# The gathers of the expert layers take their row numbers from sixteen columns that VectorE fills, and come one per piece or cycle

## The chip, the cores and the metric

The kernel runs on one core of a Trainium2 chip. The metric is the device time of one execution in microseconds (us): the median of the runs. Engines are called PE (TensorE), PEld (its weight load), DVE (VectorE), ACT (ScalarE), POOL (GpSimd) and SP (SyncE) in the profile.

## The reference, cut to what matters

Four transformer layers run in turn over 16 sequences of 256 tokens with 128 features (4096 tokens). Each has an attention and a second half, both behind a normalisation that is scaled and shifted by a condition. The second half of layer 0 and of layer 1 is a mixture of eight experts of which each token uses two. For layer 0, cut:

```python
gout = xt @ Wg.T
topv, topi = jax.lax.top_k(gout, 2)
w = jax.nn.softmax(topv, axis=-1)
comb = jnp.einsum('tke,tk->te', jax.nn.one_hot(topi, 8), w)
h = jax.nn.silu(xt @ W1[e] + b1[e]) * (xt @ W2[e] + b2[e])     # for each expert e
out = sum over e of comb[:, e] * (h @ W3[e] + b3[e])
```

Layer 1's mixture has one relu matrix product in the place of the two gated ones, and a small attention of its own before it. A token needs the results of its two experts only, which is what the kernel's lists use.

## The kernel before, in words

The tokens are in 8 blocks of 512, four blocks to a half. Layer 0 and layer 1 do their mixtures in the same four steps.

*Lists.* While the preceding attention runs, the gate of each block is worked out, and each token's row is written (scattered) by GpSimd into the list of each of its two experts, in DRAM (`rows`). When a half's lists are complete, `pieces` writes two tables: `piece`, which rows and which expert each piece has, and `origin[half]`, a 128x2x16 integer tile that says for each token in which row of the results its first and its second expert's result will stand.

*Pieces.* `sparse` runs over 2 x 23 pieces of 256 rows. For piece n it loads the rows and the expert's weights (two pieces ahead, SP queue), turns the rows (`ps_in` to `l_x`, VectorE), multiplies by the first matrices (`ps_hid` to `s`), multiplies by the second (`ps_out` to `l_o`, ScalarE) and stores the 256 results in DRAM (`done`, ACT queue).

*Sums.* `tail(blk)` calls `list_sums(blk)`: for each of four groups of 128 tokens and each of the two experts, an indirect DMA issued by GpSimd gathers 128 rows of `done` into `list_rows`, by the numbers in one column of `origin[half]` (L1619, L1620). That makes 8 gathers a block, 64 a layer. `list_rows` has room for two blocks, so block k+2's gathers wait until block k's have been summed. Then the combination weights are transposed and multiplied by the last bias (`wT`), VectorE adds the gathered rows with their weights (`acc`, in layer 1 `list_sums`), and the sums are turned and added to `x`.

*Ticks.* `tail` and the lists' functions are generators that stand in `self.later`; `advance()` steps each of them once and counts `self.tick`. In the pieces it is called three times a piece, in the attention that follows once a step (layer 1, 128 steps) or once a cycle (layer 2's attention of small heads, 138 cycles). In `list_sums` each gather is followed by one `yield`, or two in the pieces. When a tail has written its last gather, the next tail begins (it may begin when the tail two before it has summed). The first tail begins with the 25th piece, when the first half's results are out; the last four need the second half's. The attention of the next layer asks for a block's `x` through `self.tailed`, and would step the generators at once until it has it.

*Order.* Every call is written into one program; the order on each engine is then fixed when the program is compiled, from what is ready when, and with it the semaphores that carry each dependency. In the parts that matter here only the matrix products are pinned to the order in which they are written (`self.strict`); VectorE, ScalarE and GpSimd are pinned too (`self.strict_all`) in layer 0's attention and in layer 3 alone.

Names in the profile: `E` is the attention's exponentials. In layer 1 GpSimd multiplies them by `sm_inv` before TensorE transposes them into `PT`; in layer 2 GpSimd masks them (L1391) and makes `km`, the keys that TensorE starts a unit with (L1259), and `m` is their maxima (VectorE, L1383). `hb` is the normalised block that an attention starts from. `half_below` is a mask that layer 2's attention casts at its start. L230 is the line of a helper that calls VectorE, ScalarE and GpSimd; the matrix products are L273 and L276.

Of the kernel before, what the change touches and what calls it, by code (L numbers as in the profile page):

```python
# [11 lines left out]
I32 = mybir.dt.int32  # L12
# [225 lines left out]
class _Kernel:  # L238
# [522 lines left out]
    def list_tables(self, pool):  # L761
        self.in_pieces, self.listed_halves, self.tailed = False, 0, 0
        self.tails_begun = self.halves_done = self.summed = 0

        room = self.w.tile([P, 4 * BLK], F32, tag="m2", name="list_room")
        self.list_rows = self.w.tile([P, 4, BLK], F32, tag="m1", name="list_rows")
        at = 0

        def take(n):
            nonlocal at  # L770
            at += n
            return room[:, at - n : at]

        rt = take(self.t["route"].shape[-1])
        self.nc.sync.dma_start(out=rt, in_=self.t["route"])
        self.prefix, rest = rt[:, :P], rt[:, P:]
        self.first8, self.step8 = rest[:, :8], rest[:, 8:16]
        self.tri8 = rest[:, 16:80].rearrange("p (e f) -> p e f", f=8)
        self.numbers = rest[:, 80:]
        self.hots, self.two_w, self.place, self.ends, self.piece, self.origin = [], [], [], [], [], []  # L780
        two = lambda: take(32).rearrange("p (i t) -> p i t", i=2)
        eight = lambda: take(256).rearrange("p (i t e) -> p i t e", i=2, e=8)
        self.list_z, self.behind = eight(), take(NPIECE * 8).rearrange("p (k e) -> p k e", e=8)
        self.comb1 = take(NTILE * 8).rearrange("p (t e) -> p t e", e=8)
        for h in range(2):
            self.hots.append(eight())
            self.two_w.append(two())
            self.place.append(two())
            self.origin.append(pool.tile([P, 2, 16], I32, tag=f"origin{h}", name=f"origin{h}"))
            self.piece.append(pool.tile([P, 2, NPIECE], I32, tag=f"piece{h}", name=f"piece{h}"))  # L790
            ends = pool.tile([P, 8], F32, tag=f"ends{h}", name=f"ends{h}")
            self.dve.tensor_copy(ends, self.first8)
            self.ends.append(ends)
        self.room_left = room[:, at:]

    def listed(self, blks, src, chosen, pool):
# [811 lines left out]
    def list_sums(self, blk, comb, b2, wT, acc, tail):  # L1608

        half, t0 = divmod(4 * blk, 16)  # L1610
        while self.summed < blk - 1:
            yield
        w = self.two_w[half]
        g = self.list_rows[:, 2 * (blk % 2) : 2 * (blk % 2) + 2, :].rearrange("p a (u i d) -> p (a u) i d", i=2, d=P)
        for t in range(4):
            for i in range(2):
                while self.quiet:
                    yield
                of = bass.IndirectOffsetOnAxis(ap=self.origin[half][:, i, t0 + t : t0 + t + 1], axis=0)  # L1619
                self.gps.indirect_dma_start(g[:, t, i], None, self.done[half][:, :], of)  # L1620
                yield
                if self.in_pieces:
                    yield

        self.tails_begun = blk + 1
        if blk + 1 < 4 * self.halves_done:
            self.later.append(tail(blk + 1))
        for _ in range(9 if self.in_pieces else 2):
            yield
        ps = self.bank()  # L1630
        for t in range(4):
            self.turned(ps[:8, t * P : (t + 1) * P], comb[:, 4 * blk + t, :])
        self.act.copy(wT, ps[:8, :])
        yield
        ps = self.bank()
        for t in range(4):
            self.mm(ps[:, t * P : (t + 1) * P], wT[:, t * P : (t + 1) * P], b2, skip_group_check=True)
        for i in range(2):
            for t in range(4):
                v = slice(t * P, (t + 1) * P)  # L1640
                self.dve.scalar_tensor_tensor(
                    acc[:, v], g[:, t, i], w[:, i, t0 + t : t0 + t + 1], acc[:, v] if i else ps[:, v], ALU.mult, ALU.add
                )
            yield
        if self.in_pieces:
            yield
            yield
        self.summed = blk + 1
# [543 lines left out]
```

## Time and profile before

| | |
|---|---|
| median of 11 runs | 3187.99 us (3174.94 to 3197.26) |
| the profiled execution's own time | 3184.82 us, its span 3183.0 us |
| granted TensorE clock in it | 0.957 |
| pieces of layer 0 | about 813 to 958 us, 2.84 us each where nothing disturbs them |
| pieces of layer 1 | about 2103 to 2218 us, 1.98 us each |
| gathers | 128, from 881.0 to 2322.0 us, 2.6 us from issue to landing |

A line of a timeline gives the start, the duration, the engine, the line of the kernel, the operation, what it writes and reads, and in brackets how long the engine had been idle and what released it. A line of the waits gives who waited for whom, the total in us, how often, and the longest.

### The profile page before, as it was taken

How to read it: one execution, taken by the hardware profiler on the slowest of the kernel's cores; microseconds unless marked ns; L12 is line 12 of the kernel's file. 1: busy time of each engine (PE TensorE's matmuls, PEld its weight loads, DVE VectorE, ACT ScalarE, POOL GpSimd, SP SyncE). 2: the span in 40 equal slices, each digit the busy share in tenths (PEclk: the TensorE clock that was granted, in tenths of full speed). 3: DMA queues.
4: the chain of work that ended last, by engine and by line, in shares of the span. 5: the costliest groups of instructions: out<-in, count | busy, mean ns of one | idle time of the engine just before them, and what ended most of it. 6: DMA issues, size and time to landing. Idle time of an engine off the chain costs nothing. (4 is left out here: it accounts for less than half of the span.)

```text
span 3183.0 us, 51254 instructions
## 1 busy us (share of the span) xinstructions
PE 2844.0 (89%) x18502; PEld 1719.0 (54%) x18502; DVE 1950.0 (61%) x4617; ACT 1703.4 (54%) x4484; POOL 1373.5 (43%) x1239
## 2 busy tenths in 40 slices
PE   5999999888999999999978888878889898899777
PEld 3566556556886677777633333367344444555333
DVE  4777777786546676666646566423666663645564
ACT  2777776666446566666525554434244344665533
POOL 4776877772135533443320022225543231334455
PEclk9999999999999999999989999879999998999898
DMA  8040000000761000000000000156000000000000
GB/s 308 1 54 1 9 7 6 11 20 28 219 193 61 10 3 1 1 1 1 1 1 1 2 13 13 35 151 186 17 8 21 1 1 1 1 1 1 4 11 14
DMA packets 66860, 112.71 MB, mean 35 GB/s; under 512 B 10144, under 2 KB 38880, under 8 KB 66352
## 3 DMA queue, kind: packets, MB, share of 16 engines
q1 hardware_dynamic: 44848, 79.67, 8.9%
q0 software_dynamic: 8512, 17.71, 1.8%
q10 hardware_dynamic: 13248, 12.06, 1.1%
q8 instruction: 147, 2.41, 0.3%
q14 instruction: 105, 0.86, 0.1%
HBM read 70.05 MB, written 43.54 MB: 36 GB/s over the span
## 5 line engine op out<-in xcount | busy, mean ns | idle before, releaser
L230 POOL TENSOR_TENSOR E<-E,sm_inv 128x1024 f32<-128x1024 f32 (+1 forms) x241 | 407.4, 1691 | 395.4 <-PE ps_big L273 178.3
L1388 ACT ACTIVATE E<-ps_exp 128x1024 f32<-128x1024 f32 (+1 forms) x256 | 234.2, 915 | 344.3 <-PE ps_exp L273 263.8
L1383 DVE TENSOR_REDUCE m<-ps_max 128x4 f32<-128x1024 f32 (+1 forms) x246 | 268.6, 1092 | 208.9 <-PE ps_exp L273 149.4
L230 ACT ACTIVATE E<-E,sm_neg 128x256 f32<-128x256 f32 x512 | 254.1, 497 | 211.0 <-DVE sm_neg L1105 211.0
L273 PE MATMUL ps_max<-km,q 32*128 32x512 f32 (+1 forms) x984 | 265.6, 617 | 63.7 <-DVE m L1383 51.1
L276 PEld LDWEIGHTS ps_one<-w_cst,E 128*128 128x128 f32 x1792 | 205.1, 142 | 169.1 <-POOL E L230 98.7
L276 PE MATMUL ps_one<-w_cst,E 128*128 128x128 f32 x1792 | 244.9, 277 | 49.2 <-POOL E L230 36.8
L273 PE MATMUL ps_exp<-qm,q 32*128 32x512 f32 (+1 forms) x1024 | 277.8, 620 | 5.6 <-ACT E L1388 4.0
L230 DVE COPY PT<-ps_one 128x512 f32<-128x512 f32 x320 | 208.8, 685 | 97.7 <-PE ps_one L276 97.1
L273 PE MATMUL ps_big<-kT,qT 64*128 64x256 f32 (+1 forms) x2048 | 265.7, 378 | 0.0
L230 POOL DMA_INDIRECT rows<-list_rows,l_i x128 | 127.9, 999 | 262.6 <-DMA rows<-list_rows,l_i 138.9
L273 PE MATMUL ps_one<-PT,v 128*64 128x256 f32 (+1 forms) x2048 | 225.8, 363 | 3.0 <-DVE PT L230 2.7
L230 ACT ACTIVATE E<-ps_big,sm_neg 128x128 f32<-128x128 f32 (+1 forms) x512 | 208.4, 422 | 25.5 <-DVE sm_inv L230 20.0
L230 POOL TENSOR_TENSOR r_r<-r_r,r_t 128x512 f32<-128x512 f32 x128 | 162.5, 1269 | 136.3 <-DVE r_t L230 115.8
L1105 DVE CUSTOM_DVE_ANT_0 E<-ps_big,bias 128x256 f32<-128x256 f32 x512 | 186.6, 421 | 49.4 <-PE ps_big L273 38.3
L273 PEld LDWEIGHTS ps_big<-kT,qT 64*128 64x128 f32 x2048 | 166.8, 187 | 58.1 <-issue 49.5
L230 POOL DMA_INDIRECT list_rows<-done,origin x128 | 123.5, 965 | 133.2 <-issue 59.9
L273 PEld LDWEIGHTS ps_one<-PT,v 128*64 128x64 f32 x2048 | 133.1, 138 | 81.1 <-DVE sm_inv L230 13.6
L273 PEld LDWEIGHTS ps_max<-km,q 32*128 32x128 f32 x984 | 77.3, 191 | 166.5 <-DVE m L1383 81.0
L1391 POOL TENSOR_SCALAR_AFFINE_SELECT E<-E 128x512 f32<-128x512 f32 x128 | 82.6, 646 | 192.1 <-ACT E L1388 192.1
L230 DVE TENSOR_REDUCE sm_neg<-ps_big 128x4 f32<-128x512 f32 (+1 forms) x128 | 122.2, 955 | 64.3 <-PE ps_big L273 62.4
L273 PE MATMUL ps_rope<-w_a_qkv,hb 128*128 128x512 f32 x256 | 140.2, 633 | 23.6 <-ACT r_sq L230 20.2
(340 smaller groups left out, 6238.0 us busy)
## 6 DMA issues: line engine op xcount, KB each, us to landing
rows<-zeros SPq DMA_DIRECT2D x8, 2048.0 KB
list_w<-in_f_W SPq DMA_DIRECT2D x46, 257.0 KB
done<-l_o ACTq DMA_DIRECT2D x92, 128.0 KB
f_W<-in_f_W SPq DMA_DIRECT2D x27, 386.0 KB
f_room<-in_f_W SPq DMA_DIRECT2D x19, 386.0 KB
list_sums<-rows SPq DMA_DIRECT2D x46, 128.0 KB
rb_rows<-rb_d SPq DMA_DIRECT2D x1, 4088.0 KB
w_a_qkv<-in_a_qkv SPq DMA_DIRECT2D x2, 1536.0 KB
```

The lines of the kernel that those rows point to most:

```text
L230: ins = f(*args, **kw)
L273: self.ordered(self.nc.tensor.matmul(out, lhsT, rhs, start=start, stop=stop, **kw))
L276: self.ordered(self.nc.tensor.transpose(out, in_, self.c("ident")))
L1105: nc.vector.tensor_tensor_reduce(e[:, i], S[:, i], bias[g][:, i, off : off + T], 1.0, BIG, ALU.add, ALU.min, neg[:, i : i + 1])
L1383: nc.vector.tensor_reduce(o, Sm[:, :, :, :, :nk], AX.X, ALU.max, negate=True)
L1388: nc.scalar.activation(E, Se[:, :, :, :, q0:], AF.Exp, scale=scale)
L1391: nc.gpsimd.affine_select(D, D, [[0, 4], [1, P]], ALU.is_ge, 0.0, base=0, channel_multiplier=-1)
```

## The change

Sixteen columns are taken from the room of the lists' tables (`self.at16`, as integers). Before each gather VectorE copies its column of `origin` into one of them, chosen by the tick modulo 16, and the gather reads its numbers there. In the pieces a gather is now followed by three `yield`s instead of two, so that one comes per piece; elsewhere there is one per step or cycle as before.

```diff
@@ list_tables
             self.dve.tensor_copy(ends, self.first8)
             self.ends.append(ends)
+        self.at16 = take(16).bitcast(I32)
         self.room_left = room[:, at:]
@@ list_sums
             for i in range(2):
                 while self.quiet:
                     yield
-                of = bass.IndirectOffsetOnAxis(ap=self.origin[half][:, i, t0 + t : t0 + t + 1], axis=0)
+
+                at = self.at16[:, self.tick % 16 : self.tick % 16 + 1]
+                self.dve.tensor_copy(at, self.origin[half][:, i, t0 + t : t0 + t + 1])
+                of = bass.IndirectOffsetOnAxis(ap=at, axis=0)
                 self.gps.indirect_dma_start(g[:, t, i], None, self.done[half][:, :], of)
-                yield
-                if self.in_pieces:
+                for _ in range(3 if self.in_pieces else 1):
                     yield
```

## The prediction
> **What bounds the kernel now.** I read the page first, then the waits of TensorE by stage, then the timelines of GpSimd, VectorE and TensorE around the gathers. The page's first two lines say where a gain or a loss must show:
>
> ```profile
> span 3183.0 us, 51254 instructions
> PE 2844.0 (89%) x18502; PEld 1719.0 (54%) x18502; DVE 1950.0 (61%) x4617; ACT 1703.4 (54%) x4484; POOL 1373.5 (43%) x1239
> ```
>
> TensorE is the bound; VectorE and GpSimd cost time only where TensorE waits for them. The profiled execution took 3184.82 us, 3.2 us under the median of 3187.99 us. The gathers, from the view of the tile `list_rows`:
>
> ```profile
> L230 POOL DMA_INDIRECT list_rows<-done,origin x128: 946/952/1355, 881.0 to 2322.0; - x128
> ```
>
> So 128 gathers of 0.95 us stand in GpSimd's queue, between 881 and 1081 us (layer 0) and between 2159 and 2322 us (layer 1). The waits of TensorE from 965 to 1120 us, the start of layer 1's attention, are these two, the first with what released it and total, times, longest:
>
> ```profile
> PE ps_one L276 <- POOL E L230: 6.4, 4, 2.6
> PE ps_one L273 <- DVE PT L230: 2.2, 1, 2.2
> ```
>
> From 2225 to 2345 us, the start of layer 2's attention, these touch GpSimd:
>
> ```profile
> PE ps_max L273 <- POOL km L1259: 7.2, 2, 3.7
> PE ps_out L273 <- POOL E L1391: 3.9, 2, 3.2
> ```
>
> From 1120 to 1590 us, with no gathers, TensorE waits for `E` only once, 2.0 us. GpSimd's timeline shows why (start, duration, what, idle time before it):
>
> ```profile
> 1024.17 1.89 POOL L230 TENSOR_TENSOR E<-E,sm_inv 128x1024 f32<-128x1024 f32 x1 [3.05 <-DVE sm_inv L230]
> 1026.48 0.98 POOL L230 DMA_INDIRECT list_rows<-done,origin  x1 [0.42 <-DVE acc L230]
> ...
> 1035.45 0.95 POOL L230 DMA_INDIRECT list_rows<-done,origin  x1 [0.30 <-DVE sm_neg L1105]
> 1036.42 3.75 POOL L230 TENSOR_TENSOR E<-E,sm_inv 128x1024 f32<-128x1024 f32 x2
> ```
>
> Eight gathers run as one group, one per 1.256 us, 10.0 us in all, though the program writes one per step; two products of `E` wait behind them. The group was placed where it becomes ready, not where it is written. Nor is this GpSimd's habit alone. VectorE's timeline:
>
> ```profile
> 2082.78 0.22 DVE L1194 CAST half_below<-w_cst 128x128 bf16<-128x128 f32 x1
> ```
>
> This cast is written at the head of layer 2's attention, behind all 46 pieces; VectorE ran it at 2082.8 us, 154 us before TensorE first used it (2237.0 us). So the order on VectorE, too, takes an early-ready instruction far ahead.
>
> **The copies.** 128 copies of 128x1 are added. VectorE's nearest rows are a 128x4 reciprocal (0.17 us) above and the 128x1 accumulator read (0.08 us) below: 10 to 22 us of work, in an engine that idles for 39% of the span. The cover is the gaps behind TensorE (1.36 us before each `s` in the pieces). I take 2 us on the path; 0 and 22 are the ends.
>
> The places are known long before the gathers, so by the `half_below` row the first sixteen copies of a layer move far ahead. Copy 17 cannot: it writes a column that gather 1 reads, and must wait for it. That VectorE waits in this way is in its waits:
>
> ```profile
> DVE l_i L230 <- DMA rows<-list_rows,l_i: 0.2, 1, 0.2
> ```
>
> There it rewrites the index tile of a scatter and waits for the scatter's DMA. So 48 of the 64 copies of a layer are ready the moment that the gather sixteen before them ends, and will be placed there. Queued behind each on VectorE: in the pieces `s` and `l_x`, in the attentions `E`/`sm_neg`, `PT` or `m`; TensorE waits for all of these.
>
> **What such a wait costs.** It is nothing if the order was fixed with the gathers' true length. The group above says that it was not: eight gathers were put between two products of `E` that elsewhere start 3.0 to 5.7 us apart, with 1.89 us of product in it, so they were taken to fit in at most 5.7 us. They take 10.0. VectorE therefore reaches the last copy at least 4.3 us too early for each eight, and with 3.0 us assumed 7.0 us. What TensorE loses when VectorE is held is shown once:
>
> ```profile
> 980.04 4.48 DVE L230 SCALAR_TENSOR_TENSOR acc<-list_rows,list_room,acc 128x128 f32<-128x128 f32 x3
> ...
> 987.20 1.08 PE L273 MATMUL ps_one<-PT,v 128*64 128x256 f32 x8 [2.17 <-DVE PT L230]
> ```
>
> One of the three took 3.90 us instead of 0.34, so VectorE was held for 3.56 us and TensorE lost 2.17 of it, 0.61. With the low end: 4.3 x 0.61 = 2.6 us for each eight, 6 such groups a layer, 2 layers: 12 x 2.6 = **31.5 us**. The ends are 0 (lengths equal, or the slack takes all) and 12 x 7.0 = 84 us.
>
> [...]
>
> **The pacing in the pieces.** A gather takes three ticks instead of two there, and a piece makes three ticks. By the written order a tail's gathers last 24 ticks instead of 16; the second half has 24 pieces' worth, 72 ticks. Before, four tails issued their gathers in it and three summed (combination transposes at 898.4, 922.8 and 942.7 us); after, three issue and two sum. So eight gathers and one tail's sums move into the next attention, in both layers, and later tails start 8 ticks later. Nobody waits for them: layer 2 is the tighter, and asks for block 2 sixteen cycles after its first unit, when tail 2 is some four cycles done. The sums' TensorE work (0.60 + 1.15 + 0.60 us) moves and does not vanish.
>
> What it costs: one more group of eight beside attention work. In layer 1 three groups cost 6.4 us, 2.1 each; in layer 2 three groups cost 3.9 and one `km` wait of 3.7, 2.5 each. Together **+4.6 us** (0 to 10).
>
> What it saves: at the end of the first pieces one 1.0 us wait of TensorE for `wT`; at the end of the second 1.0 us for `h` and the 1.4 us that the first `ln_xc` of layer 2 waited for tail 2's `x` on GpSimd: **-3.4 us**. Late next is the chain `ln_xc`, `hb`, `km` of layer 2's start, which stays.
>
> Sum: 31.5 + 2 + 4.6 - 3.4 = +34.7 us; on the profiled execution 3219.5, on the median **3222.7 us**.
>
> **The rivals.** *It does nothing* (the copies run ahead and never wait, because the gathers' length was foreseen after all or the slack takes it): +2 + 4.6 - 3.4 = +3.2, 3191 us. For it: VectorE is busy 61% only. Against: the eight gathers between two products.
>
> *It paces, and is faster.* If the copies stay near their written place, one gather comes per step of 4.4 us, and fits the gaps of 1.1 to 3.8 us between products. Then the groups' price goes: 6.4 + 3.9 + 3.7 = 14.0 us, and with 3.4 saved and 2 spent: -15.4, 3172.6 us. It decides from the point where a copy is placed within a step or so of where it is written. Against it speaks `half_below`.
>
> *The full price*: VectorE held 7 us for each eight and TensorE with it: +84 + 3, 3275 us; the longest runs, sixteen gathers in 20 us from 881 us and thirty-two from 2159 us, both beside pieces of 2 to 3 us, speak for it.
>
> **How the numbers follow.** Waits of the size of the sum up to the full price 0.60; nothing 0.20; pacing 0.20. A measurement of this kernel can tell about 0.3% (9.6 us) from no change, so these are slower 0.60, same 0.20, faster 0.20. The range runs from the pacing case, 3172, to 3262, leaving out the top of the full price and gains beyond 15 us.
>
> **What would show it.** Right: VectorE's waits name the gathers' DMA (`list_rows`) with 30 us or more in total, 48 copies a layer or many of them; `s`, `l_x`, `PT` or `m` come late behind them; TensorE's idle time grows at 881 to 1120 and 2159 to 2345 us, and not elsewhere; gathers still run in groups 1.26 us apart. Three tails' gathers, not four, by the last piece. Wrong: no VectorE wait on a gather (nothing), or single gathers between products of `E` and no `E` waits (pacing). It is also wrong if the copies stand at their written place and GpSimd waits at each for VectorE.

## The result and the profile after

The changed kernel takes 3249.63 us (median of 8 runs, 3244.33 to 3258.03), the kernel before 3186.86 us (median of the 31 runs shown with it). The ratio is 1.0199, with a 95% interval of 1.0183 to 1.0215: slower by 2.0%, some 63 us. The forecast was 3222.7 us in a range of 3172 to 3262; the time lies inside the range, 27 us above the forecast. The profiled execution after took 3238.39 us, 53.6 us more than the one before; it lies 11 us under its median, at a granted clock of 0.956 where the other nine executions on record have 0.946 to 0.952. Differences of stretches below are differences of these two executions.

The page's first two lines after:

```profile
span 3236.6 us, 51334 instructions
PE 2853.9 (88%) x18502; PEld 1724.5 (53%) x18502; DVE 1961.7 (61%) x4745; ACT 1705.2 (53%) x4484; POOL 1375.1 (42%) x1239
```

VectorE has the 128 copies more (4745 against 4617 instructions, 11.7 us of work) and GpSimd what it had. TensorE has the same 18502 products, is busy 9.9 us longer, and stands idle 43.7 us longer. The waits of VectorE over the whole run have a row that was not there before (who waited for whom, total, times, longest):

```profile
DVE list_room L230 <- DMA list_rows<-done,list_room: 89.8, 65, 5.8
```

`list_room` here is the sixteen columns: VectorE stood 89.8 us before copies into them, each time until the DMA of a gather that reads the column had landed. 40.1 us of it lie between 880 and 1240 us, 49.7 us between 2160 and 2500 us. VectorE's timeline shows both halves of the mechanism (start, duration, what, idle time before it and its cause):

```profile
655.09 0.33 DVE L230 COPY list_room<-origin 128x1 int32<-128x1 int32 x4
...
656.01 0.79 DVE L230 COPY list_room<-origin 128x1 int32<-128x1 int32 x12
...
879.98 0.88 DVE L997 SCALAR_TENSOR_TENSOR s<-ps_hid,f_room,s 128x256 f32<-128x256 f32 x2 [1.36 <-ACT s L995]
884.57 0.15 DVE L230 COPY list_room<-origin 128x1 int32<-128x1 int32 x1 [3.72 <-DMA list_rows<-done,list_room]
885.37 0.15 DVE L230 COPY list_room<-origin 128x1 int32<-128x1 int32 x1 [0.64 <-DMA list_rows<-done,list_room]
887.24 0.15 DVE L230 COPY list_room<-origin 128x1 int32<-128x1 int32 x1 [1.71 <-DMA list_rows<-done,list_room]
887.31 0.42 DVE L1569 COPY l_x<-ps_in 128x256 f32<-128x256 f32 x1
```

The first sixteen copies run at 655 us, 225 us before the first gather and 6 us after the half's table is written (649.0 us). The seventeenth stands in front of `l_x` of a piece at 880 us, and VectorE gets to it when the first gather has been issued but has not landed. TensorE's timeline over the same time shows who pays:

```profile
880.83 1.89 PE L273 MATMUL ps_hid<-l_x,f_room 128*128 128x256 f32 x8
882.56 1.05 PE L273 MATMUL ps_out<-f_room,s 128*128 128x128 f32 x8
887.79 0.69 PE L276 MATMUL ps_in<-w_cst,f_room 128*128 128x128 f32 x2 [4.18 <-DVE l_x L1569]
888.27 3.62 PE L273 MATMUL ps_hid<-l_x,f_W 128*128 128x256 f32 x8
...
898.61 1.24 PE L273 MATMUL ps_out<-f_W,s 128*128 128x128 f32 x8 [3.27 <-DVE s L997]
```

It waits 4.18 us for `l_x`, and the eight products after that take 3.62 us where the same eight took 1.89 us just before. The windows of 4 us say why (after the length: busy us, with the count of instructions, of PE, PEld, DVE, ACT and POOL; last three: granted clock, DMA share, GB/s):

```profile
879.00:883.00 4.00, 4.00 (x27) 3.69 (x26) 0.88 (x2) 2.05 (x5) 1.95 (x2) 1.00 0.80 209
883.00:887.00 4.00, 0.61 (x6) 0.42 (x4) 0.31 (x2) 0.37 (x1) 3.04 (x4) 0.90 0.93 288
887.00:891.00 4.00, 3.21 (x9) 2.67 (x10) 1.95 (x8) 0.77 (x2) 3.09 (x4) 0.50 0.36 116
891.00:895.00 4.00, 4.00 (x21) 3.61 (x19) 0.81 (x4) 0.92 (x4) 3.09 (x4) 0.74 0.37 72
```

Before, TensorE was busy 4.00 us of 4 in each of them, at a clock of 1.00. The third of them before:

```profile
887.00:891.00 4.00, 4.00 (x27) 3.69 (x27) 2.02 (x5) 1.58 (x4) 2.86 (x3) 1.00 0.98 313
```

After, the clock is 0.50 once TensorE comes back. GpSimd's side is unchanged: the gathers still come eight in a row, one per 1.256 us, with a product of `E` ahead and one behind:

```profile
1046.78 1.90 POOL L230 TENSOR_TENSOR E<-E,sm_inv 128x1024 f32<-128x1024 f32 x1 [3.05 <-DVE sm_inv L230]
1049.09 0.98 POOL L230 DMA_INDIRECT list_rows<-done,list_room  x1 [0.42 <-DVE acc L230]
...
1058.07 0.95 POOL L230 DMA_INDIRECT list_rows<-done,list_room  x1 [0.31 <-issue]
1060.98 1.89 POOL L230 TENSOR_TENSOR E<-E,sm_inv 128x1024 f32<-128x1024 f32 x1 [1.96 <-DVE sm_inv L230]
```

The gathers' row, which was 946/952/1355 ns and ended at 2322.0 us before:

```profile
L230 POOL DMA_INDIRECT list_rows<-done,list_room x128: 946/952/1360, 880.5 to 2417.3; - x128
```

Where the 53.6 us lie is seen by cutting both executions at the same pieces of work and not at the same times. Idle is the length of a stretch less TensorE's busy time in it:

| stretch | before: length, idle | after: length, idle | idle more |
|---|---|---|---|
| to the last first product (`f_W`) of layer 0's pieces | 950.5, 103.2 | 965.0, 115.9 | 12.7 |
| on to the last `attT` product of layer 1's attention | 664.2, 16.4 | 676.3, 23.1 | 6.7 |
| on to the first `half_below` product of layer 2 | 622.3, 101.1 | 632.7, 113.9 | 12.8 |
| on to the last `half_below` product | 418.5, 42.6 | 438.4, 54.5 | 11.9 |
| on to the end (no gathers) | 527.6, 75.8 | 524.3, 75.4 | -0.4 |

Every stretch with gathers has grown, and the one without has not.

### The profile page after: what moved, and what is told of

It reads as the page before. It is cut to its first block, busy times and chain, and to the rows that moved or that the text cites. A ratio compares the mean times of both kernels' runs of the same rounds, so it can differ in the third digit from the quotient of the medians.

```text
span 3236.6 us, 51334 instructions
## 1 busy us (share of the span) xinstructions
PE 2853.9 (88%) x18502; PEld 1724.5 (53%) x18502; DVE 1961.7 (61%) x4745; ACT 1705.2 (53%) x4484; POOL 1375.1 (42%) x1239
## 5 line engine op out<-in xcount | busy, mean ns | idle before, releaser
L230 POOL DMA_INDIRECT list_rows<-done,list_room x128 | 123.9, 968 | 163.1 <-DVE acc L230 52.8
```

What stands on the lines that cost most here:

```text
L230: ins = f(*args, **kw)
```

## The experiments

The theory to be tested is that of the forecast, called W in the expectations: VectorE waits at each copy for the DMA of the gather sixteen before, and TensorE behind it. Its rivals are that the pace (three ticks, tails that end later) costs the time, or that the copies cost it by themselves, as work or in the way of GpSimd. Each ratio is against runs of the kernel before on the same chip.

### One part at a time

A column for each of the 64 copies of a layer: every copy stays and none overwrites a column in use.

```diff
-        self.at16 = take(16).bitcast(I32)
+        self.at16, self.handed = take(64).bitcast(I32), 0
...
-                at = self.at16[:, self.tick % 16 : self.tick % 16 + 1]
+                at = self.at16[:, self.handed % 64 : self.handed % 64 + 1]
+                self.handed += 1
```

> The changed kernel, but with 64 columns used in turn by a counter of the gathers, so that no copy in a layer writes a column that a gather has read. Copies and pace stay. Theory W (VectorE waits, at each copy, for the DMA of the gather sixteen before): no VectorE wait for a gather's DMA is left, and the time falls to the sum without that term, 3183 to 3197 us. Rival P (the pace of three ticks and the work moved into the attentions cost it): stays at 3240 to 3255 us. [...]

Measured: 3185.05 us, ratio 0.9998 (0.9975 to 1.002). All 128 copies are there, the pace is that of the changed kernel, and the whole loss is gone. VectorE's waits no longer name a gather's DMA. Nothing but the choice and number of columns differs from the changed kernel. So neither the copies as work nor the later tails cost what can be measured; only the waits do.

The pace alone: three ticks, and the gather reads `origin` as before.

```diff
-                at = self.at16[:, self.tick % 16 : self.tick % 16 + 1]
-                self.dve.tensor_copy(at, self.origin[half][:, i, t0 + t : t0 + t + 1])
-                of = bass.IndirectOffsetOnAxis(ap=at, axis=0)
+                of = bass.IndirectOffsetOnAxis(ap=self.origin[half][:, i, t0 + t : t0 + t + 1], axis=0)
```

> Only the pace of the change: three ticks for a gather in the pieces, the gathers read their numbers from origin as before, no copies. W: 3183 to 3195 us. P: 3235 to 3255 us. [...]

Measured: 3186.55 us, ratio 0.9997 (0.9974 to 1.0021). The one more group of eight beside layer 1's attention is there, with its price. From 965 to 1240 us TensorE's wait for `E` is now

```profile
PE ps_one L276 <- POOL E L230: 10.3, 6, 3.6
```

against 6.4 us in 4 times before, +3.9 us; from 2225 to 2460 us it is 8.6 us in 4 against 3.9 in 2. In the time it doesn't show.

The copies alone: sixteen columns, taken by a counter, and the two ticks of before. (By the tick, two ticks a gather would use only eight of the sixteen.)

```diff
-        self.at16 = take(16).bitcast(I32)
+        self.at16, self.handed = take(16).bitcast(I32), 0
...
-                at = self.at16[:, self.tick % 16 : self.tick % 16 + 1]
+                at = self.at16[:, self.handed % 16 : self.handed % 16 + 1]
+                self.handed += 1
...
-                for _ in range(3 if self.in_pieces else 1):
+                for _ in range(2 if self.in_pieces else 1):
```

> Only the copies: sixteen columns in turn by a counter of the gathers, two ticks for a gather as before. W: the waits stay, VectorE waits 70 to 110 us in all for gathers' DMA, 3230 to 3265 us. P: 3183 to 3195 us. [...]

Measured: 3259.27 us, ratio 1.0227 (1.0185 to 1.0268). VectorE's waits:

```profile
DVE list_room L230 <- DMA list_rows<-done,list_room: 91.5, 68, 8.7
```

The loss is there without the pace. W stands, and both rivals fall: the pace by this run and the one before it, the copies by themselves by the 64 columns.

### The dose

If W is right, the loss follows the number of copies that meet a gather. With 8, 16, 32 and 64 columns 56, 48, 32 and 0 copies of a layer write a column that a gather of the layer has read. Both kernels here are the changed one with another number in the place of 64 in the first diff.

> The changed kernel with thirty-two columns in turn (by a counter): 32 of a layer's 64 copies write a column that a gather has read. W: 65 x 32/48 = 43 us of loss, 3215 to 3242 us, VectorE waits for gathers' DMA of 50 to 75 us. If only the first, long run of sixteen gathers in the pieces counted: as the changed kernel, 3245 to 3255 us.

> The changed kernel with eight columns in turn (by a counter of the gathers) in place of sixteen: 56 of a layer's 64 copies write a column that a gather has read, not 48. W: the loss of 65 us against the kernel with 64 columns goes with the number of such copies, 65 x 56/48 = 75 us, so 3250 to 3285 us, with VectorE waits for gathers' DMA of 90 to 130 us. If the loss were a fixed cost of reusing columns at all: as the changed kernel, 3250 us.

The last two columns are TensorE's idle time in the profile over that of the kernel before, and the median granted clock of the runs (0.9555 to 0.957 for the kernel before).

| columns | ratio | us more ((ratio - 1) x time before) | VectorE's wait for the gathers | loss per us of wait | TensorE idle more | clock |
|---|---|---|---|---|---|---|
| 8 | 1.0206 (1.0182 to 1.023) | 66 | 94.9 us in 78 | 0.69 | 40.0 | 0.9475 |
| 16 (the change) | 1.0199 (1.0183 to 1.0215) | 63 | 89.8 us in 65 | 0.71 | 43.7 | 0.948 |
| 16 (copies alone) | 1.0227 (1.0185 to 1.0268) | 72 | 91.5 us in 68 | 0.79 | 46.1 | 0.9465 |
| 32 | 1.0141 (1.0118 to 1.0165) | 45 | 60.1 us in 48 | 0.75 | 36.6 | 0.954 |
| 64 | 0.9998 (0.9975 to 1.002) | -1 | none | - | 7.2 | 0.961 |

With 32 columns the wait is 60.1 us, and 32/48 of 89.8 is 59.9: it goes by the number of copies that meet a gather. With eight columns the same rule gives 56/48 x 89.8 = 105 us, and 94.9 were measured; the time can't be told from that with sixteen, so that run decides nothing beyond lying where W wants it.

TensorE's idle time follows the wait less closely: 36.6 us more with 32 columns, 43.7 with sixteen. The rest of the difference between the losses goes with the clock. All four kernels with these waits have a lower clock than the kernel before, and the one without has not.

### The order

The rival *it paces, and is faster* was to decide from the point where a copy is placed within a step or so of where it is written. That can be made: the copy is kept at its written place, as the matrix products are.

```diff
-                self.dve.tensor_copy(at, self.origin[half][:, i, t0 + t : t0 + t + 1])
+                self.tc.keep_in_program_order(self.dve.tensor_copy(at, self.origin[half][:, i, t0 + t : t0 + t + 1]))
```

> The changed kernel with each copy pinned on VectorE behind all that is written before it, so that it can't run ahead. W: the gather sixteen before has long landed when a copy comes, so VectorE's waits for gathers go; and the gathers come one per step, so that the groups of eight beside the attentions go too: 3165 to 3190 us. [...]

Measured: 3169.89 us, ratio 0.9943 (0.9916 to 0.997). The same 128 copies into the same sixteen columns are now 0.6% faster than before instead of 2.0% slower. GpSimd's timeline in the pieces:

```profile
890.05 0.95 POOL L230 DMA_INDIRECT list_rows<-done,list_room  x1 [1.89 <-DVE list_room L230]
892.89 0.95 POOL L230 DMA_INDIRECT list_rows<-done,list_room  x1 [1.89 <-DVE list_room L230]
```

One gather per piece of 2.84 us, each behind its copy. The wait has changed sides, from VectorE to GpSimd, whose waits now have the row

```profile
POOL list_rows L230 <- DVE list_room L230: 164.3, 80, 13.1
```

164.3 us, almost twice what VectorE lost in the changed kernel, and no cost of them shows in the time: TensorE waits for GpSimd's `E` only 0.2 us from 965 to 1240 us. VectorE waits for no gather.

Then it may be the order alone that gains, and no copies are needed. The gather pinned on GpSimd with three ticks, the copies pinned with two ticks, and, last, the kernel before with nothing but the pin:

```diff
-                self.gps.indirect_dma_start(g[:, t, i], None, self.done[half][:, :], of)
+                self.tc.keep_in_program_order(self.gps.indirect_dma_start(g[:, t, i], None, self.done[half][:, :], of))
```

> No copies: the gathers read origin, at the pace of three ticks, and each gather is pinned on GpSimd behind all that is written before it. If the gain of the pinned copies comes from breaking the groups of eight beside the attentions: groups go and TensorE's waits for E with them, 3160 to 3182 us, as with pinned copies. If it needs the hand-over by VectorE (in the pieces GpSimd has nothing else to be pinned behind, so its runs stay there): 3180 to 3192 us.

> Pinned copies with sixteen columns in turn by a counter, but two ticks for a gather in the pieces as before. If the slower pace has no part in the gain: 3160 to 3180 us. If one gather per piece matters: 3180 to 3195 us.

> The kernel before with one thing changed: each gather is pinned on GpSimd behind all that is written before it; two ticks in the pieces, no copies. If the whole gain of the pinned gathers comes from the order alone, so that neither the copies nor the slower pace have a part: 3155 to 3180 us. If the slower pace is needed for it: 3180 to 3192 us.

| kernel | ratio | median us | TensorE idle in its profile (span less busy; 339.0 before) |
|---|---|---|---|
| copies pinned, three ticks | 0.9943 (0.9916 to 0.997) | 3169.89 | 324.3 |
| gathers pinned, three ticks, no copies | 0.9919 (0.989 to 0.9947) | 3160.42 | 325.4 |
| copies pinned, two ticks | 0.9921 (0.99 to 0.9942) | 3168.75 | 329.6 |
| gathers pinned, two ticks, no copies | 0.9906 (0.9873 to 0.994) | 3158.93 | 323.9 |

All four beat the kernel before; their intervals overlap, so no order among them is shown. The last is one line of change. Its GpSimd in layer 1's attention:

```profile
1002.36 1.91 POOL L230 TENSOR_TENSOR E<-E,sm_inv 128x1024 f32<-128x1024 f32 x1
1004.42 0.98 POOL L230 DMA_INDIRECT list_rows<-done,origin  x1 [0.16 <-issue]
1008.05 1.90 POOL L230 TENSOR_TENSOR E<-E,sm_inv 128x1024 f32<-128x1024 f32 x1 [2.64 <-PE ps_big L273]
1010.09 0.98 POOL L230 DMA_INDIRECT list_rows<-done,origin  x1
```

Single gathers between products. Of TensorE's waits for `E` in the starts of both attentions none is left, and of its two for `km` one, of 3.50 us at the first unit of layer 2, as it was before (3.49); in the pieces of layer 1, where GpSimd has little else to do, the gathers still come in rows. TensorE's idle time falls by 15.1 us (339.0 to 323.9), 6.3 of them in the stretch of layer 1's attention and 5.5 in that of layer 2. The forecast's 14.0 us for these waits is thus about right, but the time falls by 30 us (0.0094 x 3195.43; 19 to 41 by the interval). In the profiles the rest is 15.0 us less busy time of TensorE for the same products, 13.5 of it in the stretch between the two attentions, where the granted clock is 0.92 against 0.90. The clocks of the runs bear that out. Among the 48 runs of the kernel before that stand beside the experiments, the time goes with the granted clock (3171 us at 0.962, 3202 at 0.952), by a fitted line 2.6 us for each 0.001. The pinned kernel's median clock is 0.963 against 0.956, by that line an estimated 18 us, and 15.1 + 18 = 33 us is close to the 30 measured. With 64 columns the clock is higher too, 0.961 against 0.957 (11 us), but the idle time is 7.2 us longer, and the medians differ by 2 us. Why the clock is higher in these kernels stays open.

## Why the prediction held, and where it was off

*The copies ran ahead.* Right: sixteen of each layer ran far ahead, in layer 0 6 us after the table was written, as the row of `half_below` had let expect.

*The copies as work, +2 us on the path.* Right within what can be measured: VectorE is busy 11.7 us longer, near the low end of the 10 to 22 expected, and with 64 columns no cost is seen (0.9998, some 7 us either way by the interval).

*Who waits, and where.* Right: the waits of VectorE name the gathers' DMA, `s` and `l_x` come late behind them, gathers stay in groups 1.256 us apart, and the loss stands in the four stretches with gathers and in no other. Off in a detail: in layer 1 it is not always the gather sixteen before. The column goes by the tick, and copy 32 there waits 2.06 us until 2223.1 us, when gather 16, issued at 2201.2 us, had long landed (at most 4.9 us from issue to landing in that profile); it waits for a nearer one.

*What such a wait costs, +31.5 us.* The mechanism is right, and the size is wrong in three places. First the wait: the sum took 4.3 us of VectorE for each eight gathers, the low end, 12 x 4.3 = 51.6 us. Measured were 89.8, 7.5 us for each eight, above even the high end of 7.0. The copies beside the first sixteen gathers of a layer make 17.6 us in each layer, 8.8 for each eight gathers; the later groups make 4.5 to 8.6. At 880 us sixteen copies come one behind the other, and most of them wait for a landing of their own, so VectorE is let go for an instruction or two at a time: TensorE waits for `l_x` (4.18 us) and later again for `s` (3.27 us).

Second the share of the wait that TensorE loses, taken from a single case as 0.61. Against the kernel with 64 columns, which has the copies and the pace without these waits, TensorE stands idle 36.5 us longer (382.7 against 346.2): 0.41 of the wait. Too small a wait and too large a share nearly cancel, 31.5 against 36.5 us, and that is luck.

Third the clock, for which the sum has no term. The median granted clock of the runs is 0.948 after and 0.956 before. By the fitted line above, the 0.008 are an estimated 21 us of the 63, which leaves 42, close to the idle time of 43.7. The kernels without these waits ran at median clocks of 0.9555 to 0.963, those with them at 0.9465 to 0.954, so the lower clock came with the waits; the windows at 883 to 895 us show one such fall behind an idle time. That the profiled executions give 53.6/89.8 = 0.60, near the 0.61, is luck too: 43.7 us of it are idle time and 9.9 longer busy time.

*The pace, +4.6 - 3.4 us.* Also mis-sized, by less. With 64 columns TensorE's idle time in the profile is 7.2 us above the kernel before, where the terms without the waits sum to 3.2. The group of eight more came in both attentions, with 3.9 us more waiting for `E` in layer 1 (10.3 against 6.4) and 4.2 in layer 2 (8.1 against 3.9), against 2.1 and 2.5 expected. The saving of 3.4 us did not come as told: TensorE's waits for `wT` and for `h` are 2.0 us each before and with 64 columns, and the first `ln_xc` of layer 2 waits 1.38 us for `x` in both. The medians show none of this (0.9997 and 0.9998).

*Three tails by the last piece.* Right: after the change 24 gathers, three tails', were issued by 932 us, and eight more from 960.7 us, when the last pieces run; before, 32 were issued by 938 us and eight more from 958.9. Two tails instead of three had begun to sum by then, and four groups instead of three then stand in layer 1's attention. The gathers of layer 1 end at 2417 us instead of 2322, and no wait of TensorE for their blocks is seen.

*The gathers' own length.* The sum has no term for longer gathers, and none was needed: their median is 952 ns with and without the copies, their longest 1360 ns against 1355, GpSimd's busy time 1375.1 us against 1373.5. The copy at 887.24 us runs inside a gather that was begun at 886.81 us and took 0.95 us like the others.

*The rivals.* "It does nothing" is what the change is with 64 columns: 3185 us, 3191 expected. "It paces" was right in its mechanism and in the point from which it decides, and became true when the order was pinned (3169.89 us, 3172.6 expected); in the changed kernel the copies were not near their written place. "The full price", 3275 us, was nearer in what VectorE loses than the forecast was, but only 63 us of the 89.8 reached the time.

## What to carry to other kernels

A small buffer that is written in turn can be a wait on its reader from the second round on, and the writer's engine stands in it with everything that is queued behind; before adding one, ask which engine will do the waiting (here VectorE's 90 us cost 63, and of GpSimd's 164 us nothing showed) and whether a buffer without reuse is to be had, which here cost nothing that could be measured. Where the order on an engine is fixed from when things are ready, writing an instruction later in the program need not delay it (the first sixteen copies ran 225 us before the first gather); here pinning did, and that single pin, on the gathers and without copies, gave 0.9%. When a wait is sized from the order of a trace, the widest gap into which the work was put gives its lower end and no more: 4.3 us for each eight gathers by that, 7.5 measured. And a wait of TensorE can cost more than its idle time (here 1.7 us more behind 4.18 us idle, at a granted clock of 0.50), so compare the granted clock of the runs as well as their times.

## What was not expected of the hardware

TensorE paid for its longer idle times twice. After 4.18 us without work its granted clock was 0.50 from 887 to 891 us and 0.74 in the next 4 us; eight products of 1.89 us took 3.62 us, which adds 1.7 us to a wait of 4.2. After the 3.27 us that end at 898.61 us the clock was 0.61 from 899 to 903 us. Layer 1's pieces show it with a short wait between two long ones; the same four products take 1.03 us without a wait:

```profile
2190.51 2.08 PE L273 MATMUL ps_hid<-l_x,list_w 128*128 128x256 f32 x4 [3.74 <-DVE l_x L1569]
...
2194.04 1.03 PE L273 MATMUL ps_hid<-l_x,list_w 128*128 128x256 f32 x4
...
2198.01 1.13 PE L273 MATMUL ps_hid<-l_x,list_w 128*128 128x256 f32 x4 [1.83 <-DVE l_x L1569]
...
2204.30 2.07 PE L273 MATMUL ps_hid<-l_x,list_w 128*128 128x256 f32 x4 [4.05 <-DVE l_x L1569]
```

Behind the waits of 3.74 and 4.05 us the granted clock was 0.50 (2190.5 to 2192.6 us and 2204.3 to 2206.4 us), behind the one of 1.83 us it was 1.00 (2198 to 2202 us). The forecast's factor of 0.61 came from a wait of 2.17 us, after which the clock stayed at 1.00 (987 to 990 us before the change), so that case could not show this cost.
